# Two-sided gated attention and LoRA block: stores of the last two tiles, the DRAM detour of x2, and all ranks of a list-scheduled kernel

## The chip, the cores and the metric

The kernel runs on one core of one Trainium2 chip. The core has five engines with instruction streams of their own: PE (matmul; PEld is its weight load), DVE (vector), ACT (scalar, activations), POOL (GpSimd) and SP, which here issues transfers only. Transfers are also issued from ACT and POOL. The metric is the time on the device in microseconds (us). Profiles show one execution of the program; its span runs from the first to the last instruction of the program.

## The reference

`x` is 2 x 1024 x 2048 in f32, `ctx` 2 x 2048 x 2048. Each of the two batches has its own context matrix, and rows are independent of each other.

```python
def fake_quant(x, scale, zp):
    q = clip(round(x / scale + zp), 0, 255)
    return (q - zp) * scale

# x1 = layernorm(x), x2 = ctx
x = x + tanh(g_xattn) * (fake_quant(layernorm(x)) @ fake_quant(ctx))
# second half, on the x just made
h = layernorm(x)
logits = h @ route_w.T            # 8 experts
best, which = top_k(logits, 1)
wh = one_hot(which) * best * (h @ A.T)     # 8 x 16 = 128 values per row
out = x + tanh(g_ffn) * (wh @ Bw)
```

## The kernel before

**Tiles and strips.** The 2048 rows of `x` are 16 tiles of 128 rows (tiles 0 to 7 are batch 0, 8 to 15 batch 1). The context of a batch is quantized in 4 strips of 512 columns; each strip has 16 chunks of 128 rows and is loaded in 4 pieces ("keys": key 0 to 15 are batch 0, 16 to 31 batch 1) of 1 MB, or in two halves where the key is in `FINE` (line 319). All matmuls of the first half are on f16 copies of the quantized integers; what the zero points make is added by a row sum of the tile (`row_sum`, line 687) and a column sum of the strip (`corr`, lines 486 to 528).

**First half, per tile** (`tokens`, line 538). The tile is loaded (L554), its mean and variance are made (on DVE if the tile is in `STATV`, L574, otherwise on ACT, L592 and L602), then the scale (L614 to L620; POOL makes the power at L624), the quantization on ACT (L638) and the clamp on DVE (L644). The quantized tile is turned either by a DMA transpose on SP (tiles in `TURN`, L665) or by PE (L675), with two copies out of PSUM (L536): the second copy is on DVE where the tile is in `COPYV`, else on ACT. The row sum is on DVE where the tile is in `SUMV` (L690), else on ACT (L692).

**Main matmul** (`group`, line 710). A group is one tile times one strip: 16 matmuls of 128x512 (L719), then the addition to x on DVE (L749 and L754, or L731 and L741 for tiles in `LATE`). The result, x2, lies where x lay. `sets` (line 288) says which tiles share a pass over the strips: 0, 1, 2 together, 3 and 4 alone, 5, 6, 7 together, 8 and 9 together, the others alone. The 64 groups are numbered 0 to 63 in that order; `first[t]` and `last[t]` are a tile's first and last group.

**Second half, per tile** (`ffn`, line 858). x2 must be turned to be multiplied by the 136 columns of A and route_w. Two ways are written: `hidden` (line 829) turns on PE (L838), copies on ACT (L852) and multiplies (L844). `hidden_moved` (line 764; tiles in `MOVE`) turns 32x32 blocks on DVE (L776), moves the blocks between partitions by transfers, sorts them on ACT (L816) and multiplies (L820). The moves are either 16 direct transfers of 64 KB from SBUF to SBUF (L794), or, for tiles in `VIA`, one store of the 1 MB to DRAM (L786) and four fetches of 256 KB (L799), which wait for that store to land. They are issued on SP; for tiles in `TWO` every second group of them is issued on ACT. Then follow the routing on DVE (L914 to L922), a small transpose (L935), its copy (L941), the output matmul (L952, two instructions for 512 columns of f32), the final addition (L960), and the store. The last tile is stored in five pieces, alternately from SP and ACT (L967); every other tile by one transfer of 1 MB from POOL (L974).

**The order of everything** is planned. Each step is a task with an engine, a booked cost and a rank; `Plan.walk` (line 76) goes through a modelled time, and on every engine takes the task of lowest rank whose operands are ready and whose buffers are free. The order that comes out is written down as the program, so each engine runs its list strictly in order and waits wherever the real time differs from the booked one. In the plan a direct move is booked as four tasks of 2.4 us on the issuing queue, a store to DRAM as 0.5, a fetch as 0.55; a transfer lands `dma_delay` = 2.5 us after its bytes at 370 GB/s.

**The tables** (lines 301 to 325) make the ranks:

- `LEAD[t]`: how many groups before its first one the tile's quantization stands (`rank = first[t] - LEAD[t]`); `XLEAD[t]` puts the load that much earlier still; `XL0` gives the rank of the loads of tiles 0 to 3 outright.
- `SUM[t]`: the row sum stands at `first[t] + SUM[t]`.
- `AFTER[t]`: the second half stands at `rank = last[t] + AFTER[t]`; the output matmul at `behind = rank + POR[t]`.
- `CTX`, `CQ`: a strip's pieces stand at (first group of the strip) - `CTX` + (part of the strip) + `CQ[key]`, for load, scale (L451 on ACT, or L462 on DVE if 2*key + half is in `VQ`) and clamp (L458, L469). `COR` places the column sum.
- Weights (`war`, `wb`; L383 to L388) are loaded at ranks 10.5 and 12.6; the loads of tiles above 3 need the second piece of strip 3 landed.

Of the kernel before, what the change touches and what calls it, by code (L numbers as in the profile page):

```python
# [42 lines left out]
class Plan:  # L43
# [11 lines left out]
    def add(self, eng, cost, rank, fn, needs=(), bufs=(), nbytes=0, alone=False, slack=0.0, parts=1):  # L55


        t = Task()
        t.eng, t.cost, t.rank, t.fn, t.nbytes = eng, cost, rank, fn, nbytes
        t.alone, t.slack, t.parts = alone, slack, parts  # L60
        t.needs, t.bufs, t.start, t.end = list(needs), list(bufs), None, None
        for b in bufs:
            b.left += 1
        self.tasks.append(t)
        return t
# [99 lines left out]
def flamingo_gated_kernel(  # L165
# [27 lines left out]
    nc = tc.nc  # L193
# [11 lines left out]
    NT = B * MT  # L205
# [57 lines left out]
    def load_scalars(queue, some):  # L263
        for i in some:
            queue.dma_start(row[:, i : i + 1], given[i].unsqueeze(0))
# [28 lines left out]
    for tiles in sets:  # L294
# [3 lines left out]
                whole[t, s] = i  # L298


    LATE = {4, 5, 6, 7}
    STATV = {0, 1, 2, 3, 5, 12, 14}
    SUMV = {5, 6, 13}
    COPYV = {7, 10, 11, 12, 13, 14, 15}
    ONES = {0}
    SUM = [8.5, 8.5, 5.5, -1, 0.5, 3.5, 8.5, 0.5, 5.5, 8.5, 5.5, 1.5, 1.5, 5.5, 3.5, 5.5]
    LEAD = [10, 10, 7, 5, 12, 8, 10, 12, 4, 7, 3, 6, 10, 2, 14, 4]
    XLEAD = [4, 4, 4, 4, 3, 0, 8, 4, 0, 3, 3, 4, 0, 0, 10, 10]
    XL0 = {0: -101, 1: -5.1, 2: -3.1, 3: 0.7}
    AFTER = [0.3, 6.2, 1.2, 0.3, 2.2, -0.8, 0.3, 5.2, 1.7, -0.8, 1.2, 2.2, 6.2, -0.8, 1.2, 0.7]  # L310
    CTX = [5, 4, 5, 3, 5, 5, 5, 2]
    COR = [3.5, 5.5, -0.5, 3.5, 3.5, -0.5, 0.5, 3.5]
    SLACK = 0.0
    VIA = {0, 1, 2, 3, 5, 6, 7, 8, 10, 11, 12}
    TWO = {0, 3, 9, 12, 14}
    XL = {11}
    PIECES = {0: 4, 1: 2, 2: 1, 3: 2}
    SPLIT = {2}
    FINE = {0, 1, 2, 3, 5, 7}
    VQ = {2, 3, 5, 6, 8, 14, 15, 17, 19, 29, 33, 39, 43, 44, 47, 51, 58, 59, 62}  # L320
    XPOOL = {7}
    WARM = [6, 12]
    POR = [1, 1.5, 0.5, 1.5, 3, 1, 4, 2, 1, 0.5, 1, 1.5, 6, 6, 0, 0.5]
    BN2 = set()
    CQ = {4: -0.1, 5: -0.7, 0: -1.4, 11: -0.1, 9: 0.5, 3: 1.3, 7: 1.0, 8: -1.7, 2: -1.0, 6: -0.6, 10: -0.2, 1: -0.5}
    SP, ACT, DVE, PE, POOL = "SP", "ACT", "DVE", "PE", "POOL"
    add = plan.add

# [5 lines left out]
        ACT, 1.5, -99, lambda: nc.scalar.activation(tab, mhalf, AF.Tanh), needs=[t_one]  # L334
    )
    t_raw = [
        add(SP, 0.9, -101.0, lambda: load_scalars(nc.sync, (0, 1)), nbytes=1, slack=3.0, parts=2),
        add(ACT, 0.9, -100.9, lambda: load_scalars(nc.scalar, (2, 3)), nbytes=1, slack=3.0, parts=2),
    ]
    t_gates = add(POOL, 1.1, -101, lambda: load_scalars(nc.gpsimd, (4, 5)), nbytes=1, slack=3.0, parts=2)  # L340
# [197 lines left out]
    def tokens(t):  # L538
# [148 lines left out]
        def row_sum():  # L687
            p = qb.ap()
            if t in SUMV:
                nc.vector.tensor_scalar(p, p, 0.0, 0.0, ALU.add, ALU.add, accum_out=rw)  # L690
# [3 lines left out]
        d = add(  # L694
            DVE if t in SUMV else ACT, 2.3 if t in SUMV else 2.1, first[t] + SUM[t], row_sum, clamps + t_turned, [qb]
        )
# [10 lines left out]

    late = LATE

# [54 lines left out]
    def hidden_moved(t, xx, hl, rank):  # L764
# [17 lines left out]
        moved = []  # L782
        if t in VIA:
            there = buf("away", f"away_{t}", [P, D], F32)
# [73 lines left out]
    def ffn(t):  # L858
        b, m = divmod(t, MT)
        end = t == NT - 1  # L860
        rank = last[t] + AFTER[t]
        xx = xb[t]
        fs = fs_[t]
        nm, sq, v, gr = (fs[:, i : i + 1] for i in range(4))
        hl = buf("hl", f"hl_{t}", [P, NC], F32)
        p = (hidden_moved if t in MOVE else hidden)(t, xx, hl, rank)
        if t not in BN2:
            junk = flat("half", f"junk_{t}", F16, D)

        def mean():  # L870
            nc.vector.tensor_scalar(  # L871
                fs[:, 4:8], acc_sums[t], -1.0 / D, None, ALU.mult, ALU.add, accum_out=nm
            )

        def inverse():

            nc.vector.tensor_scalar(v, sq, 1.0 / D, EPS, ALU.mult, ALU.add)
            nc.vector.reciprocal(v, v)
            nc.vector.tensor_scalar(gr, v, gf, None, ALU.mult)

        if t in BN2:
            bn = buf("bn", f"bn2_{t}", [P, NN, 6], F32)
            stats = [
                add(
                    DVE, 0.68, rank - 2,
                    lambda n=n: nc.vector.bn_stats(bn.ap()[:, n, :], xx.ap()[:, ts(n, NC)]),
                    [t_x2[t, n]], [xx, bn],
                )
                for n in range(NN)
            ]  # L890

            def inverse_bn():
                nc.vector.bn_aggr(fs[:, 4:6], bn.ap())
                nc.vector.tensor_scalar(v, fs[:, 5:6], EPS, None, ALU.add)
                nc.vector.reciprocal(v, v)
                nc.vector.tensor_scalar(gr, v, gf, None, ALU.mult)

            t_r2 = add(DVE, 0.7, rank - 2, inverse_bn, stats + [t_sc], [bn])
        else:
            a = add(DVE, 0.25, rank, mean, [t_x2[t, n] for n in range(NN)])  # L900
            a = add(
                ACT, 2.2, rank + 0.3,
                lambda: nc.scalar.activation(junk.ap(), xx.ap(), AF.Square, bias=nm, accum_out=sq),  # L903
                [a], [xx, junk],
            )
            t_r2 = add(DVE, 0.4, rank, inverse, [a, t_sc])
        wh = buf("wh", f"wh_{t}", [P, E, R], F32)
        top = top_[t]
        sel_b = buf("sel", f"sel_{t}", [P, 2, E], F32)

        def route():

            hv, sel = hl.ap(), sel_b.ap()
            nc.vector.tensor_reduce(top[:, 0:1], hv[:, ER : ER + E], AX.X, ALU.max)  # L914
            nc.vector.scalar_tensor_tensor(
                sel[:, 0, :], hv[:, ER : ER + E], top[:, 0:1], order8, ALU.is_equal, ALU.mult
            )
            nc.vector.tensor_reduce(top[:, 1:2], sel[:, 0, :], AX.X, ALU.max)
            nc.vector.tensor_scalar(
                sel[:, 1, :], sel[:, 0, :], top[:, 1:2], top[:, 0:1], ALU.is_equal, ALU.mult  # L920
            )
            nc.vector.tensor_tensor(  # L922
                wh.ap(),
                hv[:, :ER].rearrange("p (e r) -> p e r", r=R),
                sel[:, 1, :].unsqueeze(2).to_broadcast([P, E, R]),
                ALU.mult,
            )

        a = add(DVE, 1.25, rank - 1, route, [p, t_set], [hl, wh, sel_b])
        behind = rank + POR[t]  # L930
        pw = buf("tp", f"pw_{t}", [P, NC], F32)
        wht = buf("wht", f"wht_{t}", [ER, P], F32)
        a = add(
            PE, 0.15, behind,
            lambda: nc.tensor.transpose(  # L935
                pw.ap()[:ER, :P], wh.ap().rearrange("p e r -> p (e r)"), idf
            ),
            [a], [wh, pw],
        )
        d = add(  # L940
            ACT, 0.28, behind - 1, lambda: nc.scalar.copy(wht.ap(), pw.ap()[:ER, :P]), [a], [pw, wht]  # L941
        )
        done = []

        cuts = [(n * NC, NC) for n in range(NN)]
        if end:
            cuts[-1:] = [(D - NC, NC // 2), (D - NC // 2, NC // 2)]
        for j, (n, w) in enumerate(cuts):
            po = buf("po", f"po_{t}_{j}", [P, NC], F32)
            a = add(  # L950
                PE, 0.87 * w / NC, behind,
                lambda n=n, w=w, po=po: nc.tensor.matmul(  # L952
                    po.ap()[:, :w], wht.ap(), wb[:, n : n + w], start=True, stop=True
                ),
                [d, t_wb], [wht, po],
            )

            def finish(n=n, w=w, po=po):
                xs = xx.ap()[:, n : n + w]
                nc.vector.scalar_tensor_tensor(xs, po.ap()[:, :w], gr, xs, ALU.mult, ALU.add)  # L960

            done.append(add(DVE, 0.75 if w == NC else 0.48, behind - 0.5, finish, [a, t_r2], [po, xx]))
            if end:
                on, queue = (ACT, nc.scalar) if j % 2 else (SP, nc.sync)
                add(
                    on, 0.6, behind,
                    lambda n=n, w=w, queue=queue: queue.dma_start(  # L967
                        out[b, ts(m, P), n : n + w], xx.ap()[:, n : n + w]
                    ),
                    [done[-1]], [xx], nbytes=4 * P * w,  # L970
                )
        if not end:
            add(
                POOL, 0.6, behind, lambda: nc.gpsimd.dma_start(out[b, ts(m, P), :], xx.ap()),  # L974
                done, [xx], nbytes=4 * P * D,
            )
# [56 lines left out]
```

## Time and profile before

| what | us |
|---|---|
| median of 3 runs | 391.4 (391.33 to 391.8) |
| the profiled execution, in all | 390.69 |
| its span | 388.9 |

The page begins with the busy time of each engine, its share of the span and its instructions, and shows the span in 40 equal slices of 9.7 us: a digit is the busy share of a slice in tenths. In the chain of work that ended last, PE has 75% of the span, transfers 13%, DVE 5%. The costliest groups (line, engine, operation, count, then busy us and mean ns of one):

| group | count | busy us | mean ns |
|---|---|---|---|
| L719 PE main matmul | 1024 | 231.7 | 379 |
| L952 PE output matmul | 130 | 60.5 | 586 |
| L820 PE, x2 moved by transfers | 288 | 35.0 | 279 |
| L844 PE, x2 turned on PE | 224 | 29.1 | 280 |
| L451 ACT context scale | 28 | 53.0 | 1906 |
| L960 DVE last addition | 65 | 47.6 | 741 |

Matmuls overlap each other, so the mean of one is longer than the step from one to the next; the step is read from a run of them in the chain of waits.

The transfers by their queues (packets, MB, share of 16 engines over the span):

```profile
DMA packets 50546, 90.07 MB, mean 232 GB/s; under 512 B 21336, under 2 KB 23640, under 8 KB 46040
q1 hardware_dynamic: 46612, 70.46, 57.7%
q0 software_dynamic: 2368, 16.78, 10.6%
q10 hardware_dynamic: 1540, 2.49, 2.6%
HBM read 58.79 MB, written 23.07 MB: 210 GB/s over the span
```

q1 is SP's queue, q0 POOL's, q10 ACT's. The writes are 16 tiles of output and six tiles' detour of 1.05 MB.

### The profile page before, as it was taken

To read this page: it belongs to the slowest core of one execution; us is meant where nothing else is said; L and a number is where in the kernel's file an instruction comes from. 1 tells how busy PE (TensorE), PEld (TensorE's weight loads), DVE (VectorE), ACT (ScalarE), POOL (GpSimd) and SP (SyncE) were. 2 spreads that over 40 slices of the span, in tenths; PEclk is the share of its full clock that TensorE was granted. 3 is DMA by queue.
4 is the path that set the end of the run, shared out by engine and by line. 5 is a ranking of instruction groups with operands and counts; after the bars stand their busy time and mean duration, and the time that the engine had idled before them with its cause. 6 is when DMAs were issued, how large, how long until landed. Compare 5 with 4: busy or idle time off the path is not lost.

```text
span 388.9 us, 5343 instructions
## 1 busy us (share of the span) xinstructions
PE 371.6 (96%) x1971; PEld 215.2 (55%) x1971; DVE 308.6 (79%) x717; ACT 229.4 (59%) x224; POOL 24.1 (6%) x53
## 2 busy tenths in 40 slices
PE   6689999999999999999989999999999999999994
PEld 5344544658564644645567565545464646646662
DVE  5799999789986799589978988897668696784653
ACT  1799992979704734988859543797845322234310
POOL 3110000030001000010000100100101000000000
PEclk9999999999999999999999999999999999999999
DMA  7999999703359876887978997459649486244055
GB/s 232 398 390 386 386 368 404 253 0 56 135 241 286 263 205 173 270 321 280 328 189 290 255 422 284 170 137 185 220 141 257 143 265 169 110 116 101 2 216 217
DMA packets 50546, 90.07 MB, mean 232 GB/s; under 512 B 21336, under 2 KB 23640, under 8 KB 46040
## 3 DMA queue, kind: packets, MB, share of 16 engines
q1 hardware_dynamic: 46612, 70.46, 57.7%
q0 software_dynamic: 2368, 16.78, 10.6%
q10 hardware_dynamic: 1540, 2.49, 2.6%
q8 instruction: 15, 0.25, 0.3%
q14 instruction: 11, 0.09, 0.1%
HBM read 58.79 MB, written 23.07 MB: 210 GB/s over the span
## 4 chain that ended last, share of the span: by engine, by line
PE 75%; DMA 13%; DVE 5%; SPq 3%; ACT 2%; issue 1%; POOL 1%; DVEq 0%; ACTq 0%
PE mm L719 42%; PE po L952 14%; PE hl L820 9%; DMA st<-in_ctx_dram 8%; PE hl L844 6%; PE px L838 2%; DMA across<-away 2%; SPq L388 2%; DMA away<-turned 2%; DVE bn L574 1%; ACT q L451 1%; DMA x<-in_x_dram 1%; DVE q L462 1%; PE pq L675 1%; POOL mine L624 1%
## 5 line engine op out<-in xcount | busy, mean ns | idle before, releaser
L719 PE MATMUL mm<-q,q1t 128*128 128x512 f16 x1024 | 231.7, 379 | 2.0 <-DVE q L469 1.2
L719 PEld LDWEIGHTS <-q1t 128*128 128x128 f16 x1024 | 99.7, 98 | 121.4 <-issue 12.8
L960 DVE SCALAR_TENSOR_TENSOR x<-po,mine,x 128x512 f32<-128x512 f32 (+1 forms) x65 | 47.6, 741 | 22.2 <-PE po L952 19.5
L451 ACT ACTIVATE q<-st,raw,rs 128x2048 int16<-128x2048 f32 (+1 forms) x28 | 53.0, 1906 | 14.5 <-DMA st<-in_ctx_dram 8.9
L952 PE MATMUL po<-wb,wht 128*128 128x512 f32 (+1 forms) x130 | 60.5, 586 | 0.4 <-ACT wht L941 0.4
L903 ACT ACTIVATE junk<-x,mine 128x2048 f16<-128x2048 f32 x16 | 32.0, 2003 | 28.0 <-DVE mine L871 24.4
L749 DVE SCALAR_TENSOR_TENSOR x<-mm,sc,x 128x512 f32<-128x512 f32 x48 | 35.3, 744 | 10.9 <-PE mm L719 10.9
L638 ACT ACTIVATE q<-x,mine 128x2048 int16<-128x2048 f32 (+1 forms) x17 | 32.8, 1939 | 13.6 <-DVE mine L618 11.5
L754 DVE SCALAR_TENSOR_TENSOR x<-x,mine,corr 128x512 f32<-128x512 f32 x48 | 35.3, 749 | 1.8 <-ACT corr L527 1.0
L820 PEld LDWEIGHTS hl<-war,turned 128*128 128x128 f32 x288 | 34.7, 190 | 1.9 <-issue 0.7
L820 PE MATMUL hl<-war,turned 128*128 128x136 f32 x288 | 35.0, 279 | 0.0
L952 PEld LDWEIGHTS po<-wb,wht 128*128 128x128 f32 x130 | 23.5, 190 | 18.9 <-issue 14.0
L844 PEld LDWEIGHTS hl<-war,xt 128*128 128x128 f32 x224 | 28.0, 190 | 5.4 <-issue 2.4
L844 PE MATMUL hl<-war,xt 128*128 128x136 f32 x224 | 29.1, 280 | 1.2 <-ACT xt L852 1.2
L941 ACT COPY wht<-pw 128x128 f32<-128x128 f32 x16 | 4.2, 264 | 43.1 <-PE pw L935 43.1
L602 ACT ACTIVATE q<-x,mine 128x2048 f16<-128x2048 f32 x9 | 18.0, 1998 | 13.6 <-DVE mine L597 13.6
L692 ACT ACTIVATE q<-q 128x2048 f16<-128x2048 f16 x13 | 24.8, 1904 | 0.0
L776 DVE STREAM_TRANSPOSE turned<-x 128x512 f32<-128x512 f32 x36 | 23.5, 689 | 0.3
L852 ACT COPY xt<-px 128x512 f32<-128x512 f32 x28 | 15.5, 583 | 12.2 <-PE px L838 12.0
L816 ACT COPY turned<-across 128x1024 f32<-128x1024 f32 x18 | 17.9, 1040 | 7.6 <-DMA across<-away 5.9
L574 DVE BATCH_NORM_STATS2 bn<-x 128x6 f32<-128x512 f32 x28 | 18.1, 684 | 4.3 <-DMA x<-in_x_dram 4.3
L624 POOL TENSOR_TENSOR mine<-mine,mhalf 128x1 f32<-128x1 f32 x16 | 12.2, 763 | 146.2 <-DVE mine L609 86.2
(94 smaller groups left out, 309.1 us busy)
## 6 DMA issues: line engine op xcount, KB each, us to landing
st<-in_ctx_dram SPq DMA_DIRECT2D x26, 1024.0 KB, 8.9
out_dram<-x POOLq DMA_DIRECT2D x15, 1024.0 KB, 4.9
x<-in_x_dram SPq DMA_DIRECT2D x12, 1024.0 KB, 5.2
st<-in_ctx_dram SPq DMA_DIRECT2D x12, 512.0 KB, 10.3
away<-turned SPq DMA_DIRECT2D x6, 1024.0 KB, 5.4
across<-away SPq DMA_DIRECT2D x20, 256.0 KB, 6.3
across<-turned SPq DMA_DIRECT2D x40, 64.0 KB, 2.0
x<-in_x_dram SPq DMA_DIRECT2D x4, 512.0 KB, 10.2
```

What stands on the lines that cost most here:

```text
L451: nc.scalar.activation(part.bitcast(I16), st.ap().rearrange("p (k n) -> p k n", k=QK)[:, ts(h, n)], AF.Relu, bias=z2, scale=rs2,)
L638: nc.scalar.activation(qb.ap()[:, ts(h, hw)].bitcast(I16), xx.ap()[:, ts(h, hw)], AF.Relu, bias=nb, scale=a)
L692: nc.scalar.activation(p, p, AF.Copy, accum_out=rw)
L719: lambda k=k: nc.tensor.matmul(acc.ap(), qt.ap()[:, k, :], qb.ap()[:, k, :], start=(k == 0), stop=(k == KC - 1)),
L749: lambda: nc.vector.scalar_tensor_tensor(xs(), acc.ap(), c, xs(), ALU.mult, ALU.add),
L754: lambda: nc.vector.scalar_tensor_tensor(xs(), xs(), rs_[t], corr[:, ts(s, NC)], ALU.add, ALU.add, accum_out=ss),
L776: nc.vector.transpose(turned.ap().rearrange("p (g k i) -> p k g i", i=BLK, k=KC)[:, ts(n, BPC)], xx.ap()[:, ts(n, NC)].rearrange("p (k g j ...
L820: nc.tensor.matmul(hl.ap()[:, : ER + E], turned.ap()[:, ts(k, P)], war[:, k, :], start=(k == 0), stop=(k == KC - 1),)
L844: nc.tensor.matmul(hl.ap()[:, : ER + E], xt.ap()[:, ts(k, P)], war[:, k, :], start=(k == 0), stop=(k == KC - 1),)
L903: lambda: nc.scalar.activation(junk.ap(), xx.ap(), AF.Square, bias=nm, accum_out=sq),
L952: lambda n=n, w=w, po=po: nc.tensor.matmul(po.ap()[:, :w], wht.ap(), wb[:, n : n + w], start=True, stop=True),
L960: nc.vector.scalar_tensor_tensor(xs, po.ap()[:, :w], gr, xs, ALU.mult, ALU.add)
```

## The change

The store of the last two tiles, 14 and 15, is cut: tile 14 leaves in four pieces of 512 columns, each issued on SP as its last addition is done; tile 15 keeps its five pieces on SP and ACT alternately. All other tiles keep POOL's one transfer.

The tables are replaced. Tile 12 comes into `LATE`: its row sum and `corr` are added to x before its groups end (L731), and a group then needs one step (L741) instead of two. `VIA` within `MOVE` is 3, 5, 14 now, where it was 3, 5, 8, 10, 11, 12: tiles 8, 10, 11 and 12 go directly, tile 14 by DRAM. `TURN`, `MOVE`, `STATV`, `sets`, buffers and the booked costs stay. Every rank follows from the new numbers. `SCR` is the rank of the first scalars' load, written as a name.

```diff
-    LATE = {4, 5, 6, 7}
+    LATE = {4, 5, 6, 7, 12}
     STATV = {0, 1, 2, 3, 5, 12, 14}
-    SUMV = {5, 6, 13}
-    COPYV = {7, 10, 11, 12, 13, 14, 15}
+    SUMV = {5, 12}
+    COPYV = {0, 5, 7, 10, 11, 12, 15}
     ONES = {0}
-    SUM = [8.5, 8.5, 5.5, -1, 0.5, 3.5, 8.5, 0.5, 5.5, 8.5, 5.5, 1.5, 1.5, 5.5, 3.5, 5.5]
-    LEAD = [10, 10, 7, 5, 12, 8, 10, 12, 4, 7, 3, 6, 10, 2, 14, 4]
-    XLEAD = [4, 4, 4, 4, 3, 0, 8, 4, 0, 3, 3, 4, 0, 0, 10, 10]
-    XL0 = {0: -101, 1: -5.1, 2: -3.1, 3: 0.7}
-    AFTER = [0.3, 6.2, 1.2, 0.3, 2.2, -0.8, 0.3, 5.2, 1.7, -0.8, 1.2, 2.2, 6.2, -0.8, 1.2, 0.7]
-    CTX = [5, 4, 5, 3, 5, 5, 5, 2]
-    COR = [3.5, 5.5, -0.5, 3.5, 3.5, -0.5, 0.5, 3.5]
+    SUM = [-1, 8.5, 5.5, -1, 0.5, 2.5, 2.5, 2.5, -1, 0.5, 5.5, 1.5, 5.5, 5.5, 3.5, -1]
+    LEAD = [7, 10, 10, 7, 7, 5, 7, 12, 7, 6, 3, 6, 10, 3, 14, 3]
+    XLEAD = [4, 4, 4, 4, 3, 1, 3, 4, 0, 4, 3, 8, 3, 2, 10, 10]
+    XL0 = {0: -101, 1: -5.8, 2: -4.5, 3: 1.6}
+    AFTER = [0.3, 6.2, 0.3, -0.8, 5.2, -0.8, 0.3, 5.2, 1.7, 0.7, 2.2, 1.7, 6.2, 0.3, 4.2, 2.2]
+    CTX = [6, 4, 5, 3, 5, 5, 5, 2]
+    COR = [3.5, 5.5, -0.5, 3.5, -0.5, 2.5, 5.5, 3.5]
     SLACK = 0.0
-    VIA = {0, 1, 2, 3, 5, 6, 7, 8, 10, 11, 12}
-    TWO = {0, 3, 9, 12, 14}
+    VIA = {1, 2, 3, 5, 6, 7, 9, 14}
+    TWO = {0, 4, 6, 9, 12}
     XL = {11}
     PIECES = {0: 4, 1: 2, 2: 1, 3: 2}
     SPLIT = {2}
-    FINE = {0, 1, 2, 3, 5, 7}
-    VQ = {2, 3, 5, 6, 8, 14, 15, 17, 19, 29, 33, 39, 43, 44, 47, 51, 58, 59, 62}
+    FINE = {0, 1, 2, 3, 6, 7}
+    VQ = {3, 5, 6, 8, 14, 15, 17, 19, 23, 39, 43, 44, 47, 51, 57, 58, 61, 62, 63}
     XPOOL = {7}
     WARM = [6, 12]
-    POR = [1, 1.5, 0.5, 1.5, 3, 1, 4, 2, 1, 0.5, 1, 1.5, 6, 6, 0, 0.5]
+    SCR = -101.0
+    POR = [0, 1, 1.5, 1, 0, 1, 4, 2, 1, 1, 6, 0.5, 6, 0.5, 2, 0.5]
     BN2 = set()
-    CQ = {4: -0.1, 5: -0.7, 0: -1.4, 11: -0.1, 9: 0.5, 3: 1.3, 7: 1.0, 8: -1.7, 2: -1.0, 6: -0.6, 10: -0.2, 1: -0.5}
+    CQ = {4: -0.9, 5: -0.7, 0: -1.4, 11: -0.8, 9: 0.5, 3: 1.3, 7: 1.0, 8: -1.8, 2: -0.4, 6: -0.5, 10: -0.2, 1: -0.5}
...
-        add(SP, 0.9, -101.0, lambda: load_scalars(nc.sync, (0, 1)), nbytes=1, slack=3.0, parts=2),
+        add(SP, 0.9, SCR, lambda: load_scalars(nc.sync, (0, 1)), nbytes=1, slack=3.0, parts=2),
...
-            if end:
-                on, queue = (ACT, nc.scalar) if j % 2 else (SP, nc.sync)
+            if t >= NT - 2:
+                on, queue = (ACT, nc.scalar) if end and j % 2 else (SP, nc.sync)
...
-        if not end:
+        if t < NT - 2:
```

## The prediction

> **What bounds the kernel now.** I read the page first (busy shares and the 40 slices), then the chain that ended last, then what TensorE (PE) waited for, then the timeline at each of those waits.
>
> ```profile
> PE 371.6 (96%) x1971; PEld 215.2 (55%) x1971; DVE 308.6 (79%) x717; ACT 229.4 (59%) x224; POOL 24.1 (6%) x53
> PE   6689999999999999999989999999999999999994
> PEclk9999999999999999999999999999999999999999
> DMA  7999999703359876887978997459649486244055
> ```
>
> PE is busy nearly everywhere at full clock; the transfers are full only in the first seven slices (to 68 us). A busy PE need not be fully fed, so I counted its work by the shortest unit of each kind in the chain: 1024 main matmuls at 17.91/83 = 0.216 us (221), 130 of L952 at 1.72/4 = 0.43 (56), 512 of L820 and L844 at 3.71/32 = 0.116 (59), 112 transposes of L838 at 0.87/8 = 0.109 (12), 112 of L675 at 0.89/16 = 0.056 (6), 23 column sums at 0.22 (5). That is 359 us. The span is 388.9; the first of these starts at 12.9, and the last ends at 383.6, 5.3 before the end. So only 388.9 - 359 - 12.9 - 5.3 = some 11 us are lost while PE could work. The list of PE's waits says where:
>
> ```profile
> PE pq L675 <- DVE q L644: 2.5, 4, 1.1
> PE pw L935 <- DVE wh L922: 1.4, 1, 1.4
> PE mm L719 <- DVE q L469: 1.2, 2, 0.7
> PE hl L844 <- ACT xt L852: 1.2, 1, 1.2
> PE mm L719 <- DVE q L458: 0.7, 1, 0.7
> PE po L952 <- ACT wht L941: 0.4, 1, 0.4
> ```
>
> (us in all, times, longest.) Placed by the timeline: L675 and L719 <- L469 wait between 13 and 32 us, L719 <- L458 at 70, L844 at 200, the two others at the very end. In the windows from 100 to 355 us PE is busy 253.78 of 255: the order of everything there is loose, except at 200. The wait at 70 is ended by the last piece of the first context half:
>
> ```profile
> 56.91 11.31 DMA st<-in_ctx_dram
> 68.24 2.10 ACT q L451
> 70.37 0.70 DVE q L458
> 71.11 2.75 PE mm L719 x12
> ```
>
> (start, us.) Transfers set the time up to 71 us, PE from there on. So an edit pays only where it takes a PE wait away, and costs only where it makes one.
>
> **Lists that change little.** An index in VQ is 2*key+h, and h = 1 exists only for keys in FINE. So of VQ's edits one is real: key 1's first half is scaled on ACT, no longer on DVE. COPYV counts only for tiles not in TURN: tile 0's second copy goes to DVE. TWO counts only in MOVE: tiles 3 and 14 lose ACT's half of the issues, tile 4 gets it. Among the loads of the first half, sorted by their new ranks, 1b comes before 2a, 3b before strip 1's first piece, strip 2's last piece before strip 1's last; the rest, and the whole second half's CTX, stand as before. SCR equals the old constant. PE's work is the same.
>
> **The start (13 to 71 us).** Key 1's first half costs DVE 0.81 us (16.38 in the timeline) and ACT 1.23 (the 10.04 row). Tile 0's second copy costs ACT 1.00 and DVE 0.69. DVE gains 0.1, ACT loses 0.2; but ACT idles 1.79 us before 18.27 and can run that scale from 15.5 instead of DVE from 16.38, so its clamp (0.43) ends by 17.2, not 18.6. The two matmul waits for L469 at 18.6 and 19.8 (1.2 us, 1.5 counted by starts) can shrink to nothing. From 31.7 to 70 PE runs without a break, so it would reach the wait at 70 earlier by that much, and that wait ends with a transfer that did not move: the gain turns into a longer wait, unless tile 3's matmuls, whose operands are there, are put in front. Tile 3's own chain gets a lower rank (LEAD 5 to 7). Bounds: 0 (all absorbed) and -2.4 (1.5 + the 0.9 at 70); worse, one more clamp late, +0.8. I take -0.5, near the absorbed end, since the row shows a transfer ending the chain.
>
> **The wait at 200.** Tile 5's rows go by DRAM and land late; ACT stands in its order before the sort, and the copy of another tile stands behind it:
>
> ```profile
> 199.37 1.99 ACT L816 COPY turned<-across 128x1024 f32<-128x1024 f32 x2 [3.47 <-DMA across<-away]
> 201.27 0.58 ACT L852 COPY xt<-px 128x512 f32<-128x512 f32 x1
> 201.90 1.19 PE L844 MATMUL hl<-war,xt 128*128 128x136 f32 x8 [1.22 <-ACT xt L852]
> ```
>
> Tile 5 stays in VIA, and its AFTER and the second half's CTX stay. What lies around it moves: tile 8's rank is 25 instead of 28, tile 6's row sum goes to ACT (1.90) with rank 23.5 instead of 29.5, and COR of three strips changes. So the same order there is as likely as another. Bounds 0 and -1.4; I take half, -0.7.
>
> **Moves without DRAM.** Tiles 8, 10, 11 and 12 give up one store and four fetches for 16 issues on SP; tile 14 goes the other way. The rows:
>
> ```profile
> away<-turned SPq DMA_DIRECT2D x6, 1024.0 KB, 5.4
> across<-away SPq DMA_DIRECT2D x20, 256.0 KB, 6.3
> across<-turned SPq DMA_DIRECT2D x40, 64.0 KB, 2.0
> 138.99 11.62 SPq L794 DMA_DIRECT2D across<-turned  x16
> ```
>
> Tile 4's 16 issues take 11.62 us, and the last lands 2.0 later: 13.6 us. By DRAM, tiles 8, 10, 11, 12 took 14.9, 15.2, 11.5 and 12.0 from the store's issue to the last landing (259.5 to 274.4, 284.0 to 299.2, 306.5 to 318.0, 318.7 to 330.7). So the new way is 1.3 and 1.6 us sooner for two, 2.1 and 1.6 later for two. The sort (about 1 us each half) ends 1.4 to 1.5 us before PE's first matmul on tiles 8, 10 and 11, and 4 before tile 12's, and PE waits at none of them, so sooner gains nothing. Later by 2.1 and 1.6 falls on tile 11, 0.6 past its cover, and on tile 12, inside it; PE's new order may leave more or less cover. I take 0, since the four differences nearly cancel; bounds 0 and +2.4 (rival 2). Behind these issues on SP stand the transposes of L665 (289.0, 297.4; the tiles they feed start at 316 and 341) and the x load at 267.7: ten us later they are still in time. The spared DRAM traffic (four tiles fewer, one more: 3 MB each way) lies where the transfers have room (DMA share 0.79 in 284 to 300, 0.66 in 318 to 332): 0.
>
> [...]
>
> **Row sums, tile 12 and ranks.** A row sum is 2.28 us on DVE, 1.90 on ACT; two leave DVE, one comes. Tile 12 joins LATE: one L731 of 2.35 us takes the place of four L754 of 0.75, so DVE gains 0.6; but its sums can't leave PSUM until the row sum and L731 are done, with rank 53.5 for the row sum where its groups stand at 48 to 51. Cover: DVE is busy 10 to 12 of 14 to 16 us in that stage (11.82 in 284 to 300), so it takes the row sum whenever that is ready, and there are four PSUM banks for groups of 3.5 us each; without it PE would wait for one L731, 2.35. SUM, COR, POR, AFTER reorder work on engines that are busy 79% and 59%. Cover: PE's queue of ready matmuls. Without it, one misplaced ACT or DVE step costs what the one at 200 costs, 1.4. I take 0 for all of this; bounds 0 and +2.4.
>
> **The end.** Tile 14's store was one POOL issue at 378.81. Now four SP issues of 0.36 each follow its four L960 results (374.3 to 378.5). SP has nothing else from 354.7 to 382.65, so tile 15's pieces are not held up: the last is issued at 385.1 either way and lands 2.6 later. 0; if SP were late, at most 4 x 0.36 = +1.4. Tile 14's way by DRAM: its turns end at 345, + 5.4 + 1.8 + 6.3 = 358.5, sort 2.0: ready at 360.5, against a sort begun at 361.7 before. The last wait (pw <- wh) stays: the new ranks put tile 14's output matmuls and tile 15's L844 at the same 65.2, and tile 14's stand first, so nothing is left to fill it. 0.
>
> **Sum.** -0.5 - 0.7 = -1.2 us on the span, 388.9 to 387.7. The profiled execution took 390.69 in all, 1.8 more than its span, and the runs' median is 391.4; the difference goes on the median: **390.2 us**.
>
> **Rivals.**
> 1. *No net change, about 391.3.* The start's gain is absorbed at 70, and the wait at 200 stays. For: both are ended by transfers that keep their places. Chance 0.19.
> 2. *Slower, about 393.8: direct moves come late.* The plan books 2.4 us for four issues (9.6 a tile); the row says 11.62, 2.0 later than booked. Where the plan puts the sort and PE's L820 right behind the landing, the 1.4 us that stood between them does not cover it: 0.6 us of PE wait at each of tiles 8, 10, 11, 12 is 2.4. It decides from the point where a move ends over 1.4 us late. Against: tiles 4 and 13 went directly before, and PE did not wait for them. Chance 0.31. [...]
> 3. *Faster by 3.5, 387.9.* Tile 3's matmuls fill the wait at 70, so the start counts in full (2.4), and the wait at 200 goes (1.4), less some 0.3 left over. For: the operands of tile 3 are there from about 50 us. Against: it needs several orders to fall well. Chance 0.10.
>
> **How the numbers follow.** Forecast 0.40, lying in 389.3 to 390.7. A measurement of this kernel tells 0.2% (0.8 us) from no change. Faster: 0.40 less a little that ends within 0.8, plus 0.10: 0.48. Slower: 0.31. Same: 0.21, rival 1 and that little. The range takes the forecast, rival 1, most of rival 2 and the near side of rival 3: 388.3 to 393.8.
>
> **What would show it.** In the new profile: the mm <- L469 waits near 18 us gone, and the wait at 70 longer (absorbed) or gone (filled); the ACT gap before L816 near 199 with or without a PE wait for xt behind it; for tiles 8, 10, 11, 12 sixteen L794 issues of about 11.6 us, and no PE wait at L820 (right) or four short ones (rival 2); the last store issued about 1.5 us after the last PE matmul. A PE wait over 2 us anywhere between 80 and 355 would make the prediction wrong.

## The result and the profile after

| kernel | median us | ratio to before, 95% interval |
|---|---|---|
| before, 10 runs | 391.37 | |
| changed, 10 runs | 389.1 | 0.9939 (0.9914 to 0.9963) |
| changed, 12 runs beside experiments | 388.87 | 0.9944 (0.9919 to 0.9968) |

The change makes the kernel 0.6% faster: 0.0061 x 391.4 is 2.4 us, with 1.4 to 3.4 inside the interval. The prediction had 1.2. The changed kernel's profiled execution took 389.57 us, with a span of 387.8; before it was 390.69 and 388.9. So this pair of profiles shows 1.1 us, less than the medians do: the execution profiled before lay 0.7 us under its median, the changed one 0.5 over its own.

The page of the changed kernel, its first lines and its transfers; then the lines of what PE waited for that the argument uses (us in all, times, longest). The line of SCR shifts the line numbers behind it by one: L720 is L719 of before.

```profile
PE 372.8 (96%) x1971; PEld 216.2 (56%) x1971; DVE 305.8 (79%) x712; ACT 232.5 (60%) x226; POOL 24.2 (6%) x52
DMA packets 51123, 86.93 MB, mean 224 GB/s; under 512 B 21912, under 2 KB 24216, under 8 KB 47128
HBM read 55.64 MB, written 19.92 MB: 195 GB/s over the span
```

```profile
PE mm L720 <- DVE q L459: 1.1, 1, 1.1
PE pq L676 <- DVE q L654: 1.0, 1, 1.0
PE hl L821 <- ACT turned L817: 0.9, 2, 0.7
PE mm L720 <- ACT q1t L537: 0.4, 2, 0.3
PE hl L845 <- ACT xt L853: 0.4, 1, 0.4
```

Busy times are the same within 1.4%; 3 MB less goes each way to DRAM. In the list of waits the two at the end (pw <- DVE wh, po <- ACT wht) are gone, the one on L845 at 200 is smaller, the one at 70 is longer, and a new one has come: L821, the multiplication by way of transfers, waits for ACT's sort.

To see where the time went, I took every step from one PE matmul's start to the next, less the unit of its kind (0.216, 0.43, 0.116, 0.109, 0.056 us, as in the prediction), and added what is left by stage; the first column is the time of the first of these matmuls and what is lost from there to 32 us. The last column runs from the modelled end of the last matmul to the end of the span. Kernels with names of their own are the experiments below.

| us | start, and lost to 32 | lost 32 to 72 | near 128 | near 200 | 206 to 355 | last waits | behind PE |
|---|---|---|---|---|---|---|---|
| before | 18.6 | 0.9 | 0 | 1.5 | 0 | 2.2 | 4.5 |
| changed | 17.2 | 2.1 | 0.5 | 0.7 | 0.9 | 0 | 4.9 |
| changed, again | 17.5 | 1.7 | 0.4 | 0 | 0.9 | 0 | 4.8 |
| e10_store_only | 18.3 | 1.4 | 0.3 | 1.1 | 0 | 2.2 | 4.3 |
| e8_por14_only | 17.9 | 1.4 | 1.2 | 0 | 0 | 0.7 | 6.5 |
| e9_por14_and_store | 18.4 | 1.4 | 0.6 | 1.2 | 0 | 0.7 | 4.3 |
| e2_store_back | 17.3 | 1.6 | 0.3 | 0 | 0.7 | 0 | 6.5 |
| e6_two_12 | 18.1 | 1.5 | 0.7 | 0 | 0 | 0 | 4.7 |

Three things are read from it. The columns at 128 and 200 change by themselves: e10 runs the same orders as before on PE, DVE and ACT, and has 0.3 and 1.1 there where before had 0 and 1.5; e8 has 1.2 and 0. So a difference of one such column between two profiles says little. The two columns at the left scatter too: four profiles with the start of before have 17.9 to 18.6 and 0.9 to 1.4, four with the changed start 17.2 to 18.1 and 1.5 to 2.1, so only their means count (18.3 to 17.5, and 1.3 to 1.7), and a cell there is good to some 0.4 us. The two columns at the right do not behave so: 2.2, 0.7 or 0, and 4.3 to 4.9 or 6.5, by what the kernel does there. The end of the kernel before, in its timeline (start, us, engine, line):

```profile
378.81 0.53 POOL L974 DMA_DIRECT2D out_dram<-x  x1 [6.34 <-DVE x L960]
380.02 0.33 PE L935 MATMUL pw<-idf,wh 128*128 128x128 f32 x1 [1.37 <-DVE wh L922]
380.70 3.71 PE L952 MATMUL po<-wb,wht 128*128 128x512 f32 x10 [0.36 <-ACT wht L941]
```

The end of the changed kernel:

```profile
376.09 0.53 POOL L975 DMA_DIRECT2D out_dram<-x  x1 [11.30 <-DVE x L961]
377.49 0.27 PE L936 MATMUL pw<-idf,wh 128*128 128x128 f32 x1
377.60 5.32 PE L953 MATMUL po<-wb,wht 128*128 128x512 f32 x14
377.94 6.05 SPq L968 DMA_DIRECT2D out_dram<-x  x7
```

Fourteen output matmuls run in one piece: four of tile 14's and the ten of tile 15. While tile 15 is routed (376 to 377.5) PE works on tile 14's. POOL's issue at 376.09 is tile 13's store; tile 14 leaves by four of SP's seven issues.

### The profile page after: what moved, and what is told of

The parts are those of the page before. It is cut to its first block, busy times and chain, and to the rows that moved or that the text cites. A ratio compares the mean times of both kernels' runs of the same rounds, so it can differ in the third digit from the quotient of the medians.

```text
span 387.8 us, 5398 instructions
## 1 busy us (share of the span) xinstructions
PE 372.8 (96%) x1971; PEld 216.2 (56%) x1971; DVE 305.8 (79%) x712; ACT 232.5 (60%) x226; POOL 24.2 (6%) x52
## 4 chain that ended last, share of the span: by engine, by line
PE 71%; DMA 15%; SPq 5%; DVE 3%; ACT 2%; ACTq 1%; issue 1%; POOL 0%; DVEq 0%
PE mm L720 41%; PE po L953 12%; PE hl L821 9%; PE hl L845 6%; DMA st<-in_ctx_dram 6%; DMA x<-in_x_dram 4%; DMA across<-away 4%; SPq L389 3%; PE px L839 2%; DMA away<-turned 2%; SPq L445 1%; ACT q L452 1%; ACT turned L817 1%; ACTq L795 1%; PE pq L676 1%; DVE turned L777 1%
## 5 line engine op out<-in xcount | busy, mean ns | idle before, releaser
L720 PE MATMUL mm<-q,q1t 128*128 128x512 f16 x1024 | 231.9, 379 | 1.7 <-DVE q L459 1.1
L720 PEld LDWEIGHTS <-q1t 128*128 128x128 f16 x1024 | 99.7, 98 | 121.1 <-issue 12.7
L452 ACT ACTIVATE q<-st,raw,rs 128x2048 int16<-128x2048 f32 (+1 forms) x29 | 54.4, 1887 | 14.7 <-DMA st<-in_ctx_dram 11.2
L750 DVE SCALAR_TENSOR_TENSOR x<-mm,sc,x 128x512 f32<-128x512 f32 x44 | 32.4, 745 | 13.6 <-PE mm L720 13.2
L821 PEld LDWEIGHTS hl<-war,turned 128*128 128x128 f32 x288 | 34.5, 190 | 3.5 <-ACT turned L817 1.9
L821 PE MATMUL hl<-war,turned 128*128 128x136 f32 x288 | 35.2, 280 | 0.9 <-ACT turned L817 0.9
L755 DVE SCALAR_TENSOR_TENSOR x<-x,mine,corr 128x512 f32<-128x512 f32 x44 | 32.4, 749 | 1.7 <-ACT corr L528 0.9
L845 PEld LDWEIGHTS hl<-war,xt 128*128 128x128 f32 x224 | 27.7, 190 | 3.8 <-issue 1.7
L845 PE MATMUL hl<-war,xt 128*128 128x136 f32 x224 | 29.1, 280 | 0.4 <-ACT xt L853 0.4
L817 ACT COPY turned<-across 128x1024 f32<-128x1024 f32 x18 | 17.9, 1043 | 18.7 <-DMA across<-away 9.1
L693 ACT ACTIVATE q<-q 128x2048 f16<-128x2048 f16 x14 | 26.7, 1908 | 0.0
L593 ACT ACTIVATE q<-x 128x2048 f16<-128x2048 f32 x9 | 17.2, 1912 | 8.4 <-DVE mine L700 5.1
```

The source lines that it names most:

```text
L452: nc.scalar.activation(part.bitcast(I16), st.ap().rearrange("p (k n) -> p k n", k=QK)[:, ts(h, n)], AF.Relu, bias=z2, scale=rs2,)
L693: nc.scalar.activation(p, p, AF.Copy, accum_out=rw)
L720: lambda k=k: nc.tensor.matmul(acc.ap(), qt.ap()[:, k, :], qb.ap()[:, k, :], start=(k == 0), stop=(k == KC - 1)),
L750: lambda: nc.vector.scalar_tensor_tensor(xs(), acc.ap(), c, xs(), ALU.mult, ALU.add),
L755: lambda: nc.vector.scalar_tensor_tensor(xs(), xs(), rs_[t], corr[:, ts(s, NC)], ALU.add, ALU.add, accum_out=ss),
L821: nc.tensor.matmul(hl.ap()[:, : ER + E], turned.ap()[:, ts(k, P)], war[:, k, :], start=(k == 0), stop=(k == KC - 1),)
```

## The experiments

Each ratio is to the kernel before on the same chip, from 4 (e3), 6 (e6, e9), 9 (e11) or 12 executions; intervals are 95%.

**Tile 14's ranks at the end put back** (e1_tail_ranks_back, on the changed kernel).

```diff
 AFTER[14]: 4.2 -> 1.2
 POR[14]:   2   -> 0
```

> The changed kernel with tile 14's AFTER and POR as before (1.2 and 0), all else as changed. Theory A (most of the gain is PE's last wait, filled by tile 14's output matmuls): tile 15's four L845 stand last again, PE waits 1.5 to 2.2 us before the last output matmuls, and the time is 1.5 to 2.2 us above the changed kernel's, near 391. Rival B (the gain comes from the start, the moves without DRAM and the store by pieces): 389.1 as the changed kernel, within 0.5.

Measured: 1.0039 (1.0013 to 1.0065), median 392.58. The last wait is back (2.2 us), as theory A said, but the two ranks move more than that: PE waits another 1.2 us for ACT's sort at 347, and the last matmuls run at half clock for a while (below). Slower than A's 391 by these; rival B, within 0.5 of 389.1, falls.

**The store alone put back** (e2_store_back, on the changed kernel).

```diff
-            if t >= NT - 2:
+            if end:
...
-        if t < NT - 2:
+        if not end:
```

> The changed kernel with tile 14 stored by POOL's one transfer again; PE, DVE and ACT run the same order. The prediction's step (the store by pieces is worth nothing): within 0.4 us of the changed kernel, the last store landing within 0.3 us of the same distance from the last PE matmul. Rival B (the store by pieces empties the transfers for tile 15's end): 0.5 to 1.5 us slower, the last landing later.

Measured: 0.9973 (0.9949 to 0.9997), median 390.01. That is 0.3% above the changed kernel's 0.9939 and 0.9944, some 1.2 us; the intervals overlap, so the time alone does not settle it, but the trace does: from PE's end to the span's end it is 6.5 us, not 4.9, and the last store takes 4.6 us from issue to landing (382.3 to 386.95), where it took 2.8 in the changed kernel (383.7 to 386.45). Rival B holds: in the changed kernel the store by pieces is worth 1.6 us by the two profiles, and the prediction's "0" is wrong there.

**The order of the end alone** (e8_por14_only, on the kernel before): one number.

```diff
 POR[14]: 0 -> 3.6
```

> The kernel before with one number changed: POR of tile 14 is 3.6, not 0, so its output matmuls stand behind tile 15's L844. Theory A: the wait of 1.5 + 0.6 us before the last output matmuls goes, 1.5 to 2.2 us faster than before, about 389.4. Rival B: the wait only moves (tile 14's last additions and store then end later), within 0.5 us of before.

Measured: 1.0002 (0.9981 to 1.0022), median 391.22. Theory A falls as it stood, and rival B was right: the wait on the routing is gone (2.2 to 0.7), PE's last matmul ends at 382.6 instead of 384.4, and the span ends at 389.2. Its end shows why:

```profile
377.32 5.32 PE L952 MATMUL po<-wb,wht 128*128 128x512 f32 x14
378.38 4.97 DVE L960 SCALAR_TENSOR_TENSOR x<-po,mine,x 128x512 f32<-128x512 f32 x7 [0.22 <-PE po L952]
380.29 0.53 POOL L974 DMA_DIRECT2D out_dram<-x  x1 [8.06 <-DVE x L960]
380.88 3.21 SPq L967 DMA_DIRECT2D out_dram<-x  x3
```

Tile 14's matmuls now run up to tile 15's, so POOL's 1 MB store starts at 380.29, where it was 378.81, and tile 15's pieces are issued from 380.88 on, where it was 382.65. They share the transfers. The last of them is issued at 383.4 and lands at 388.0: 4.6 us, where before it took 2.6.

**Both, and the store alone** (e9_por14_and_store and e10_store_only, on the kernel before): the diff of e2 the other way round, with and without POR[14] = 3.6.

> The kernel before with two things: POR of tile 14 at 3.6 and tile 14 stored in four pieces on SP. Theory C (the two need each other: filling PE's last wait makes tile 14's store late, and only the pieces keep it out of tile 15's way): PE's last matmul ends 1.8 us earlier and the span ends 4.5 to 4.9 us behind it, so 1.4 to 1.8 us faster than before. Rival D (the end is worth nothing, the gain is in the start and the moves): within 0.4 us of before, as with POR alone.

> The kernel before with tile 14 stored in four pieces on SP and nothing else; PE, DVE and ACT keep their order. Theory C and the prediction's step: 0, within 0.4 us of before, since POOL's store was done before tile 15's began. Rival B (pieces are better by themselves): 0.5 to 1.5 us faster.

Measured: both 0.9950 (0.9932 to 0.9969), median 388.56; the store alone 1.0006 (0.9978 to 1.0033), median 390.59. With both, ACT's last store lands 2.8 us after its issue (383.85 to 386.65), and only 4.3 us lie behind PE. Theory C holds in the time. In this one profile PE ends 0.9 us earlier, not 1.8: the last wait is 1.5 shorter, but 0.6 is lost near 128, where before lost nothing. The four kernels are a square: neither 1, order alone 1.0002, store alone 1.0006, both 0.9950. Neither part has a gain of its own; the gain is in the pair.

**The start alone** (e4_start_only, on the kernel before): the changed kernel's XL0, FINE, VQ, CQ, CTX[0], COPYV of tile 0, and LEAD, SUM, AFTER, POR of tiles 0 to 3.

```diff
+ XL0 = {0: -101, 1: -5.8, 2: -4.5, 3: 1.6}; CTX[0] = 6; FINE, VQ, CQ as changed
+ LEAD[0, 2, 3] = 7, 10, 7; SUM[0] = -1; AFTER[2, 3] = 0.3, -0.8; POR[0..3] = 0, 1, 1.5, 1
```

> The kernel before with the changed kernel's tables of the start alone (XL0, CTX and CQ of the first half, FINE, VQ, COPYV of tile 0, LEAD, SUM, AFTER and POR of tiles 0 to 3). The prediction's step (absorbed): PE loses 1.6 us less before 32 us and 1.2 more at 70, net 0 to -0.5 us. Rival (the start counts in full): -1.6 us.

Measured: 0.9988 (0.9963 to 1.0013), median 390.23: 0.5 us, with no change inside the interval. In its trace the first column of the table is 17.4 (1.2 less than in the one profile of before, 0.9 less than the mean of 18.3), the second 1.8 (0.9 and 0.5 more). What goes is the wait for L469: 1.2 us in all five profiles with the start of before (before, e8, e9, e10, e12), 0.2 here. "Absorbed" fits, and the rival's 1.6 lies just outside the interval's 1.4; the 0.5 itself is not clear of 0. The chain of waits of the changed kernel shows the same end of that stretch as before (start, us):

```profile
59.71 8.65 DMA st<-in_ctx_dram
68.39 2.10 ACT q L452
70.52 0.70 DVE q L459
71.26 2.75 PE mm L720 x12
```

The last piece lands at 68.4, where it landed at 68.2; PE is there sooner and waits longer.

**wb's load behind the context** (e5_wb_late, on the changed kernel): `t_wb` needs the last context piece of the first half.

```diff
-        t_wb = add(SP, 0.6, 12.6, ..., after, nbytes=4 * ER * D)
+        t_wb = add(SP, 0.6, 12.6, ..., [t_ctx[0, NN - 1, NQ - 1]], nbytes=4 * ER * D)
```

> The changed kernel with the load of wb (1 MB) put behind the last context piece of the first half. Theory (transfers set the time up to 71 us, PE behind that): the last piece lands some 2.7 us earlier (1 MB at 390 GB/s), the PE wait of 1.2 to 2.1 us near 70 goes, 1 to 2 us faster than the changed kernel. Rival (PE is the bound there and the wait is only slack): the wait turns up elsewhere before 100 us, within 0.4 us.

Measured: 0.9973 (0.9951 to 0.9996), median 389.36, not faster than the changed kernel. The last piece was there 2.4 us earlier (ACT starts on it at 66.04, not 68.39), as expected, but PE then waits twice: 1.6 us for that piece, and 0.9 for the sums of the weights, which DVE makes only now. The rival holds: near 70 several things come ready together, and taking the first away shows the next. (The plan's order also differs from 66 us on, so this is not that one wait alone.)

**VIA and TWO put back** (e3_via_back, on the changed kernel), and **the moves alone** (e12_moves_only, on the kernel before).

```diff
 e3:   VIA = {0, 1, 2, 3, 5, 6, 7, 8, 10, 11, 12}   TWO = {0, 3, 9, 12, 14}
 e12:  VIA = {1, 2, 3, 5, 6, 7, 9, 14}              TWO = {0, 3, 9}
```

> The changed kernel with VIA and TWO as before (tiles 8, 10, 11, 12 by DRAM, 14 directly). The prediction's step (the moves are worth 0): within 0.5 us of the changed kernel, or 0.9 faster where the wait at 318 goes. Rival 2 of the prediction (direct moves cost PE waits): 1 to 2 us faster. The opposite (less DRAM traffic pays): 0.5 to 1.5 us slower, with PE waits at L821.

> The kernel before with the changed VIA alone (tiles 8, 10, 11, 12 direct, tile 14 by DRAM; all moves on SP but tile 3's). PE's order is the same up to 260 us. The prediction's step: 0, within 0.5 us of before, no PE wait at L820. Rival 2 of the prediction: 1 to 2.4 us slower, with PE waits of some 0.6 us at L820 for tiles 8, 10, 11, 12.

Measured: e3 1.0152 (1.0132 to 1.0172), median 396.32, and none of the three expectations. But nothing of the moves costs it: its trace has one stretch in which PE loses 7.0 us, before tile 8, the first of the tiles that it sends by DRAM again:

```profile
239.17 0.38 PE L521 MATMUL cs<-sum,ones 128*128 128x512 f16 x1
243.54 1.09 PE L839 MATMUL px<-idf,x 128*128 128x128 f32 x4 [4.00 <-DVE x L755]
```

TWO also names tiles 3 and 4, and PE's order differs from 157 us on; at 239 it has transposes whose operands DVE has not made. (Two waits are 5.3 of the 7.0; the rest is the half clock told of below.) Without these 7.0 the span of 394.7 would be 387.7, about the changed kernel's. As a test of the moves e3 is spoiled, and e12, whose PE order is that of before up to 279 us, takes its place: 1.0020 (0.9991 to 1.0049), median 392.39. The moves without DRAM are worth nothing, perhaps a little less than nothing; one PE wait appears at L820 (0.6 us by the list of waits, tile 10, at 298). Of rival 2's four, one came.

**Tile 12's moves on SP alone** (e6_two_12, on the changed kernel). PE's order is the same.

```diff
-    TWO = {0, 4, 6, 9, 12}
+    TWO = {0, 4, 6, 9}
```

> The changed kernel with tile 12 taken out of TWO: all its moves are issued on SP, none on ACT. Theory (ACT's issues of tile 12's moves stand in front of tile 11's sort): ACT starts that sort some 3 us earlier, PE's wait at L821 near 318 (0.5 to 0.9 us) goes, 0.3 to 0.9 us faster than the changed kernel. Rival (the moves land late by themselves): the wait stays, tile 12's moves end later too, 0 to 1 us slower.

Measured: 0.9902 (0.9870 to 0.9934), median 387.54, beside 388.87 of the changed kernel on the same chip: the fastest of all. In the changed kernel's timeline ACT issues four transfers of tile 12, which takes it 3.47 us, before it sorts tile 11; PE waits:

```profile
314.35 3.47 ACTq L795 DMA_DIRECT2D across<-turned  x4
318.01 1.99 ACT L817 COPY turned<-across 128x1024 f32<-128x1024 f32 x2 [4.87 <-DVE x L961]
319.11 3.16 PE L821 MATMUL hl<-war,turned 128*128 128x136 f32 x25 [0.68 <-ACT turned L817]
```

In e6 the issues are gone from ACT, the sort begins at 316.04, and PE goes on without a wait:

```profile
316.04 1.98 ACT L817 COPY turned<-across 128x1024 f32<-128x1024 f32 x2
317.89 2.36 PE L821 MATMUL hl<-war,turned 128*128 128x136 f32 x19
```

The theory holds: 0.9 us of PE's loss goes in the trace, though the sort starts only 2.0 us earlier, not 3. The medians differ by 1.3; the two intervals overlap, but run against run five of e6's six executions (386.97 to 388.06) are faster than all twelve of the changed kernel (388.24 and up). The rival falls: tile 12's last moves are issued at 326.7 on SP, as late as at 326.8 on ACT before, and its sort begins at 329.0 as then.

**The start and the end together** (e11_start_and_end: e4, POR[14] = 3.6 and the store by pieces, nothing else) and the changed kernel again.

> The kernel before with the start's tables of the changed kernel, POR of tile 14 at 3.6 and tile 14 stored in pieces; no change of VIA, TWO or any rank of tiles 4 to 13. If the end and the start are all that the change is worth: 0.5 + 2.0 us, 0.993 to 0.995 of the kernel before, level with the changed kernel. If the moves without DRAM and the other ranks pay too: 0.5 us or more slower than the changed kernel.

> The changed kernel itself once more, beside the three others on one chip: 0.992 to 0.996 of the kernel before; its trace shows whether the PE waits at 70 (2.1 us), 128 (0.5), 200 (0.7) and 318 (0.9) come again.

Measured: 0.9931 (0.9908 to 0.9955), median 388.74, and 0.9944 (0.9919 to 0.9968), median 388.87. They are level: the pair at the end and the start are enough for the whole gain, and the rest of the change nets to nothing that these runs can tell. The start's own part is not resolved: the pair alone (0.9950) lies inside the same intervals. The nothing is a sum: by the profiles the changed kernel loses 0.9 at 318, where e11 loses nothing, and e11 still has 0.7 of the last wait, where the changed kernel has none. The changed kernel's waits at 70, 128 and 318 came again (1.7, 0.4, 0.9), the one at 200 did not.

## Why the prediction was right, and where not

**The bound was right.** PE sets the time behind 71 us, and only its waits count, together with what the last stores add behind it. 389.1 lies in the range of 388.3 to 393.8, and faster had the highest chance. (The prediction counted on telling 0.8 us from no change; with 10 runs the interval reaches 1.0 us to each side.) That it came out faster by the forecast's terms is in good part luck: of the -1.2 us, -0.5 is not clear of 0 in e4 and -0.7 is a wait that changes by itself, while the part that the runs show clear of noise, the end, stood at 0.

**The size was not: the step that failed is "The end", taken at 0 in both its parts.** The prediction read that tile 14's output matmuls "stand first, so nothing is left to fill" the last wait. The tie at 65.2 was there, the conclusion was wrong: e1 puts the two ranks of tile 14 back, and the wait is back. In the trace, the changed plan moves tile 14's x2 before tile 13's (the store to DRAM is issued at 333.6, tile 13's moves from 342.5), so tile 13's transpose stands at 368.9 only, and its four output steps take turns with L845's parts. Tile 14's transpose follows at 372.1, two of its output steps at 375.8, and two were still to do when tile 15's routing began. The wait of 2.2 us went to 0. The other part, the store by pieces, is 0 by itself on the old order, as predicted (e10, 1.0006), but the price was taken with the old order: with the new one POOL's store would have run into tile 15's (6.5 us behind PE in e2, 4.9 in the changed kernel). The prediction had the two rows of that cover ("one POOL issue at 378.81", and SP free until 382.65) and did not ask what becomes of it when the order in front changes. Together the two are 0.5% (e9), 1.95 us of 390.6, where 0 stood.

**The start** (-0.5, "near the absorbed end"): in line with e4's 0.9988, whose interval takes in 0, and by the mechanism named. The wait for L469 shrank from 1.2 to 0.2, and the wait at 70, ended by a transfer that had not moved, grew: by the means of four profiles each, 0.8 less before 32 us and 0.4 more behind, both good to a few tenths.

**The wait at 200** (-0.7): 1.5 to 0.7 in the first pair of profiles, but that is luck. It was 1.5, 1.1, 0 and 1.2 in kernels with PE's order of before (before, e10, e8, e9). It varies from one execution to the next; half of it was as good as any number.

**The moves** (0): right in sum (e12, 1.0020). The 16 issues of tiles 10 and 11 took 12.44 and 11.00 us in the changed kernel, about the row's 11.62. But the working missed one: tile 12 is direct now and in TWO, so 8 of its 16 issues are ACT's, not SP's, as the prediction had it. They stand in front of tile 11's sort and cost 0.9 us of PE at 318. That is rival 2's kind of wait, at one tile, by another cause: ACT's issues, not the landing.

**Row sums, tile 12 in LATE** (0): no PE wait of theirs appears. Not tried alone.

**The medians moved more than the first pair of profiles.** Each profile is one execution, and these two lay 0.7 under and 0.5 over their medians. The clock (last section) may be a part of the scatter: with PE's last wait in the order, some executions also run their last matmuls at half clock. The four experiments with that wait (e1, e4, e10, e12) spread over 4.0 to 5.0 us from run to run, the changed kernel, e6, e8, e9 and e11 over 1.4 to 3.3, but e2, also without it, over 4.2. How often the clock halves there is open.

## What to carry to other kernels

Price two edits at the same place together: an edit worth nothing because something covers it may be what another edit needs when that one takes the cover away, and a square of four kernels shows it. At the end of a kernel, look for work of the tile before that can fill the last routing, and then see that this tile's store does not meet the last one's. Transfers issued from an engine that also computes stand in its order; count them there, before the copies behind them.

## What the runs showed of the hardware

The granted clock of PE can halve for 3.4 us behind a short wait. In e4 PE waits 1.4 us for the routing and 0.4 for the copy, and then:

```profile
378.86 0.33 PE L935 MATMUL pw<-idf,wh 128*128 128x128 f32 x1 [1.37 <-DVE wh L922]
379.55 5.40 PE L952 MATMUL po<-wb,wht 128*128 128x512 f32 x10 [0.36 <-ACT wht L941]
```

The same ten matmuls take 3.71 us in the kernel before (its line at 380.70, above). Over 376 to 380 and 380 to 384 us, the windows of e4 (busy time and, in brackets, count of each engine, then granted clock, share and GB/s of the transfers) show the clock:

```profile
376.00:380.00 4.00, 2.28 (x12) 1.49 (x11) 2.38 (x7) 0.27 (x1) 0.53 (x1) 1.00 0.31 133
380.00:384.00 4.00, 4.00 (x7) 1.64 (x6) 1.50 (x3) 0.00 (x0) 0.00 (x0) 0.58 0.50 199
```

Five profiled kernels have that last wait (before, e1, e4, e10, e12); e1 and e4 show the halved clock behind it, the others do not, and none of the kernels without the wait shows it at its end before the last matmul. In e3 the clock fell to 0.50 from 242 to 248, from within the wait of 4.2 us that began at 239.

The wait is the same in all five, 1.4 and 0.4 us; what differs is where it falls. Count stretches of 3.41 us back from the moment when the clock changes: in e1 and e4 both parts of the wait lie in one stretch, in which PE is busy for 1.63 and 1.69 us, and the next stretch is at half clock. In before, e10 and e12 they are divided between two, with 2.04 to 3.06 us busy in each, and the clock stays. No limit follows from this: a stretch with 1.58 us busy at the end of e2 was followed by full clock, with PE idle.

The Trainium skill (TensorE: Matmul & The Clock Gate, Part 1) has a free-running window of about 3.4 us in which activity is judged, and two states, half and full clock; the two values and the length agree. By the rule of the same page (Why this matters for your kernels) only idle gaps over about 3 us need be avoided; here waits of 1.4 and 0.4 us were followed by it in two profiles of five, so by these runs shorter gaps may count too, and such a wait at the end may cost 1.7 us more (5.40 against 3.71). That the wait causes it was not tried by itself.
